# A graph layer on one core: one edge tile in 20 fetched row by row in place of one in 28, and another lead for GpSimd's gathers

## The chip, the core and the metric

The kernel runs on one core of one Trainium2 chip. The metric is the device time of one execution in microseconds; the number of a kernel is the median of its runs. Five engines work side by side, each with its own queue of instructions taken strictly in order: TensorE (PE in the profile; its weight loads have a row of their own, PEld), VectorE (DVE), ScalarE (ACT), GpSimd (POOL) and SyncE (SP). SP, ACT and POOL also issue DMAs; in this kernel ACT does almost nothing else after the first stage.

## What is computed

One layer of a graph network with relations, over 12,500 nodes of 256 features and 212,500 edges that are sorted by their target:

```python
h = jnp.maximum(_layernorm(x, axis=-1), 0.0)
hx = jnp.einsum('ni,rio->rno', h, weight)        # 8 relations
agg = jax.ops.segment_sum(hx[edge_type, src], dst, num_segments=N)
out = x + agg * 0.5**0.5 + h_bias + (h @ loop_weight) * 0.5**0.5
```

## The kernel before

The kernel sums the normalized rows `h[src]` of a target's edges first, for each relation apart, and multiplies by the weights afterwards. The edges are cut into 1583 tiles of at most 128; two tiles make a unit, 128 units make a block of 256 tiles.

**Edge tiles.** For each tile, the 128 rows `h[src]` of 1 KB must be brought from HBM into `msg`, one row to a partition. `edge_sums` (L953) then multiplies them by a one-hot matrix `oh`, which VectorE makes (L935), in four matmuls (L972; 32-bit data), and `add_sums` (L988) lets VectorE add the result of a unit to the ring `acc` of sums (L998). The buffers of `msg` hold 66 tiles.

**Two ways to bring the rows.** Most tiles are *gathered*: `gather` (L871) issues one indirect DMA on GpSimd (L885), which takes the 128 indices of the tile from a column of `gidx`. The others are *fetched*: `single_rows` (L855) picks tile t if `t % SINGLE == SINGLE - 1`, if it lies in block 1 or later, and if `t + AHEAD < NT` (64 and 1583). `begin_fetch` (L860) cuts such a tile into four parts of 32 rows, two for SP's queue and two for ACT's. `load_sources` (L897) loads the 32 row offsets of a part into registers of that engine (L900, a TENSOR_LOAD in the profile), and `fetch_row` (L907) issues a DMA of 1 KB for each row (L908). TensorE waits for a fetched tile's 128 rows on one of four counters ahead of the tile's first matmul (L969).

**Group products.** The nodes stand in 98 groups of 128. When a group's sums are complete, `product` (L1145) multiplies them by the weights (L1154, 36 matmuls a group), and `finish` (L1164) adds them to the rows of `x`, stores four groups at a time on SP (L1173) and begins a group further on. The rows `hr` and `xr` of later groups are loaded on SP (L1104), four groups at a time. The edge indices of the next block are loaded on SP too (L380), and small rows of each block, `spans`, on ACT from block 2 on (L392).

**What sets the order.** The program is written out in one loop over the tiles t (L1316), and each engine takes its own instructions in that order.

- The gathers run ahead of the sums: at step t, tiles up to `goal(t)` (L892) are gathered. The lead is `max(NEXT, AHEAD - max(0, t - NARROW) // SLOPE)`: 64 tiles up to t = 170, then one tile less every 5 tiles, down to `NEXT` = 8 at t = 450, and 8 from there on. A second bound (`STARTED`, `STEEP`) holds it down in the first tiles. Each gather waits for the sums of the last unit ahead of it in the program (L889, "no faster than the sums").
- A fetch begins at step t for tile t + `FAR` = t + 36, or when the gathers reach the tile, where their lead is longer than that. Its parts are put in two lists, to be taken from 8 steps later (`HOLD`), and each step takes up to `FETCH` = 4 entries (a load or a row) from each list (L920). A tile is 66 entries a list, about 17 steps. A buffer of `msg` is given out in the order of these calls, and a row waits until the tile that had the buffer before is summed.
- The stores and loads of the groups, of the indices and of the spans stand between the rows on SP's and ACT's queues where the loop puts them.

Before the loop and in its first part, the rows of x are normalized and written to `h32` in HBM; the first 100 gathers take x itself and normalize in place.

Of the kernel before, what the change touches and what calls it, by code (L numbers as in the profile page):

```python
# [55 lines left out]
STEEP = 2  # L56
NARROW = 170
SLOPE = 5
NEXT = 8

SINGLE = 28
FETCH = 4
SOURCES = 32
BY_SP = (0, 2)
# [175 lines left out]
def kernel(  # L240
# [20 lines left out]
    NT = plan.NT  # L261
# [36 lines left out]
    def place_of(t):  # L298
        u, i = divmod(t, PAIR)
        half = 0 if PAIR * u + 1 == NT else PAIR - 1 - i  # L300
        return u // P, half, u % P


    with ExitStack() as main:
# [550 lines left out]
        def single_rows(t):  # L855

            return (t % SINGLE == SINGLE - 1 and place_of(t)[0] and t + AHEAD < NT
                    and state["h32"] is not None and t // QUAD * QUAD >= state["h32"] + LATE)
# [33 lines left out]
        def goal(t):  # L892

            lead = max(NEXT, AHEAD - max(0, t - NARROW) // SLOPE)
            return min(t + lead + 1, STARTED + STEEP * (t // PAIR * PAIR))

        def load_sources(t, r0, engine):  # L897
# [302 lines left out]
        with tc.manual_schedule():  # L1200
# [115 lines left out]
            for t in range(NT):  # L1316
# [3 lines left out]
                while gathered < min(NT, goal(t)):  # L1320
                    gather(gathered)
                    gathered += 1
# [122 lines left out]
```

## Time and profile before

| what | value |
| --- | --- |
| median of 3 runs | 1996.98 us (1995.14 to 1998.15) |
| the profiled execution | 1995.13 us |
| its span, first to last instruction | 1993.4 us |
| PE busy | 1779.7 us (89%) |
| PEld busy | 1557.2 us (78%) |
| DVE busy | 1378.2 us (69%) |
| POOL busy | 1461.3 us (73%) |
| ACT busy | 136.1 us (7%) |
| mean granted TensorE clock | 0.959 |

How to read it. Times are microseconds from the start of the span; durations of single instructions are often given in nanoseconds. A group's row reads: line, engine, operation, output<-input by the program's names, xcount | busy time, mean ns of one | idle time of the engine ahead of them, and what ended most of that idle time. "issue" there is time in which the engine waited for nothing that the profile shows. A timeline row reads: start, duration, engine, line, operation, names, xcount [idle time before <- what ended it]; neighbouring instructions of one line are merged, and SPq or ACTq stands for an issue queue. A waits row reads: who <- whom: us in total, times, longest. A windows row reads: from:to, length, then busy us (xcount) of each engine that takes part, the granted clock, the share of the DMA engines and GB/s. Issuing a DMA or loading registers is not counted as busy, so ACT and SP can be full while these rows show nothing; their timelines show it.

### The profile page before, as it was taken

How to read it: one execution, taken by the hardware profiler on the slowest of the kernel's cores; microseconds unless marked ns; L12 is line 12 of the kernel's file. 1: busy time of each engine (PE TensorE's matmuls, PEld its weight loads, DVE VectorE, ACT ScalarE, POOL GpSimd, SP SyncE). 2: the span in 40 equal slices, each digit the busy share in tenths (PEclk: the TensorE clock that was granted, in tenths of full speed). 3: DMA queues.
4: the chain of work that ended last, by engine and by line, in shares of the span. 5: the costliest groups of instructions: out<-in, count | busy, mean ns of one | idle time of the engine just before them, and what ended most of it. 6: DMA issues, size and time to landing. Idle time of an engine off the chain costs nothing. (4 is left out here: it accounts for less than half of the span.)

```text
span 1993.4 us, 39889 instructions
## 1 busy us (share of the span) xinstructions
PE 1779.7 (89%) x10171; PEld 1557.2 (78%) x10171; DVE 1378.2 (69%) x3288; ACT 136.1 (7%) x243; POOL 1461.3 (73%) x1563
## 2 busy tenths in 40 slices
PE   2458999999999988999999999999999999899998
PEld 2347899899978876888878887878877887787986
DVE  6779767779856777656569666668766667765752
ACT  6764200000000000000000000000000000000000
POOL 7677777777767777777777777777777777777774
PEclk9559999999999999999999999999999999999999
DMA  8993434444444544444444444444444344444432
GB/s 269 354 289 98 143 106 138 141 136 120 139 119 118 150 130 114 136 130 123 140 119 142 131 119 139 131 129 139 132 121 142 109 141 131 117 142 118 130 106 77
DMA packets 157314, 279.57 MB, mean 140 GB/s; under 512 B 34799, under 2 KB 107864, under 8 KB 157080
## 3 DMA queue, kind: packets, MB, share of 16 engines
q0 software_dynamic: 73824, 201.69, 34.7%
q1 hardware_dynamic: 75896, 72.34, 11.7%
q10 hardware_dynamic: 7360, 2.97, 0.8%
q8 instruction: 80, 1.31, 0.3%
q14 instruction: 154, 1.26, 0.2%
HBM read 251.26 MB, written 25.60 MB: 139 GB/s over the span
## 5 line engine op out<-in xcount | busy, mean ns | idle before, releaser
L885 POOL DMA_INDIRECT msg<-h,gidx x1438 | 1364.7, 949 | 470.0 <-issue 353.8
L972 PEld LDWEIGHTS ps<-oh,msg 128*128 128x128 f32 x6332 | 995.2, 197 | 344.8 <-DMA msg<-h,gidx 206.5
L972 PE MATMUL ps<-oh,msg 128*128 128x176 f32 (+1 forms) x6332 | 1107.2, 305 | 176.2 <-DMA msg<-h,gidx 99.4
L1154 PE MATMUL po<-w,acc 128*128 128x256 f32 x3136 | 883.1, 386 | 9.4 <-DVE acc L998 9.4
L998 DVE TENSOR_TENSOR acc<-acc,ps 128x352 f32 x792 | 409.9, 518 | 369.9 <-PE ps L972 357.8
L1154 PEld LDWEIGHTS po<-w,acc 128*128 128x128 f32 x3136 | 532.1, 192 | 42.8 <-DVE acc L998 11.4
L935 DVE TENSOR_TENSOR oh<-fixed,cols 128x704 f32<-128x704 f32 x397 | 349.2, 880 | 0.0
L1036 DVE SCALAR_TENSOR_TENSOR acc<-types,pt 128x256 f32<-128x256 bf16 (+1 forms) x688 | 247.5, 413 | 85.0 <-PE pt L1018 79.8
L885 POOL DMA_INDIRECT msg<-in_x_dram,gidx x100 | 94.8, 948 | 38.8 <-issue 30.3
L1154 PE MATMUL po<-wl,self_t 128*128 128x256 f32 x392 | 111.7, 409 | 3.4 <-DVE acc L998 1.7
L1154 PEld LDWEIGHTS po<-wl,self_t 128*128 128x128 f32 x392 | 72.0, 205 | 12.9 <-DVE acc L998 2.5
L823 ACT ACTIVATE msg<-msg,shift,rstd 128x256 f32<-128x256 f32 x100 | 50.7, 586 | 4.2 <-DVE shift L820 3.4
L823 ACT ACTIVATE xt<-xt,shift,rstd 128x256 f32<-128x256 f32 x98 | 50.0, 587 | 7.0 <-DVE shift L820 5.6
L1167 DVE TENSOR_TENSOR xr<-xr,po 128x256 f32<-128x256 f32 x98 | 40.5, 414 | 13.3 <-PE po L1154 12.5
L793 DVE BATCH_NORM_STATS2 stats<-xt 128x6 f32<-128x256 f32 x98 | 34.3, 412 | 19.1 <-DMA xt<-in_x_dram 18.3
L1090 DVE CAST types<-pt 128x512 bf16<-128x512 f32 x22 | 15.2, 692 | 44.8 <-PE pt L1086 44.8
L1023 DVE COPY self_t<-pt 128x256 f32<-128x256 f32 x98 | 40.8, 416 | 6.8 <-PE pt L1018 5.5
L1018 PE MATMUL pt<-ident,hr 128*128 128x128 f32 x196 | 38.1, 277 | 7.5 <-DMA hr<-h 6.4
L1168 DVE TENSOR_TENSOR xr<-xr,po 128x256 f32<-128x256 f32 x98 | 41.2, 421 | 3.4
L429 DVE TENSOR_SCALAR moves<-fixed 128x271 int32<-128x271 int32 (+1 forms) x90 | 40.5, 451 | 3.1 <-DVE acc L998 2.1
L431 DVE COPY_PREDICATED fixed<-moves,fixed 128x311 int32<-128x311 int32 (+14 forms) x90 | 38.0, 422 | 3.1
L793 DVE BATCH_NORM_STATS2 stats<-msg 128x6 f32<-128x256 f32 x100 | 34.2, 410 | 0.0
(154 smaller groups left out, 321.1 us busy)
## 6 DMA issues: line engine op xcount, KB each, us to landing
msg<-h SPq DMA_DIRECT2D x2880, 1.0 KB
msg<-h ACTq DMA_DIRECT2D x2880, 1.0 KB
msg<-h,gidx POOLq DMA_INDIRECT x1438
xt<-in_x_dram SPq DMA_DIRECT2D x24, 512.0 KB
h<-xt SPq DMA_DIRECT2D x24, 512.0 KB
xr<-in_x_dram SPq DMA_DIRECT2D x24, 512.0 KB
hr<-h SPq DMA_DIRECT2D x24, 512.0 KB
out_dram<-xr SPq DMA_DIRECT2D x24, 512.0 KB
```

The lines of the kernel that those rows point to most:

```text
L429: nc.vector.tensor_single_scalar(m, packed[:, :n], 1 << (bit + k), op=ALU.bitwise_and)
L793: in_run("stats", nc.vector.bn_stats(stats[:n, k, :], row), row is rows_[-1])
L823: nc.scalar.activation(row, row, AF.Relu, bias=shift[:n, j : j + 1], scale=rstd[:n, j : j + 1])
L885: i = nc.gpsimd.indirect_dma_start(out=msg[t], out_offset=None, in_=table[:, :], in_offset=bass.IndirectOffsetOnAxis(ap=gidx[b][:, at : at ...
L935: j = nc.vector.tensor_tensor(o[:, k : k + v, :i, :], iota_f.unsqueeze(1).unsqueeze(1).to_broadcast([P, v, i, C]), of.unsqueeze(3).to_broa ...
L972: j = nc.tensor.matmul(ps[:, c, :width], m[:, c * P : (c + 1) * P], o[:, :width], start=(i == 0 and c == 0), stop=(end and c == KC - 1))
L998: i = nc.vector.tensor_tensor(a, a, ps, op=ALU.add)
L1023: nc.vector.tensor_copy(got["self", g][:, :, :n], pst[:, :, :n])
L1036: i = nc.vector.scalar_tensor_tensor(acc[:, :, r, s0 : s0 + n], of, float(r + 1), pst[:, :, :n], op0=ALU.is_equal, op1=ALU.mult)
L1154: i = nc.tensor.matmul(got["out", g][:n], lhs, rhs, start=(r == R and c == 0), stop=(r == R - 1 and c == KC - 1))
L1167: nc.vector.tensor_add(rows_[:n, k, :], rows_[:n, k, :], outs[g % 2][:n, 1, :])
L1168: nc.vector.tensor_add(rows_[:n, k, :], rows_[:n, k, :], got["out", g][:n])
```

## The change

Three constants and one line in `goal`:

```diff
-NEXT = 8
-
-SINGLE = 28
+NEXT = 24
+CLOSE = 8
+
+SINGLE = 20
@@ def goal(t):
             lead = max(NEXT, AHEAD - max(0, t - NARROW) // SLOPE)
+            lead = min(lead, max(CLOSE, (NT - t) // SLOPE))
             return min(t + lead + 1, STARTED + STEEP * (t // PAIR * PAIR))
```

The fetched tiles are those with t % 20 == 19, where they were those with t % 28 == 27. The gathers' lead falls from 64 as before, but to 24 tiles, which it has from t = 370 on. Near the end it is (1583 - t) // 5, below 24 from t = 1464 on and 8 from t = 1539 on. Everything else stays, the entries a step, the distance of 36 tiles and the four counters too.

## The prediction, made before the result was known

> **What bounds the kernel now.** I read the page first (its costliest groups and its DMA issues), then a stretch of the timeline, then the waits of all engines, then busy time by window, and last the timelines of the two issue queues, SP's and ACT's.
>
> ```profile
> L885 POOL DMA_INDIRECT msg<-h,gidx x1438 | 1364.7, 949 | 470.0 <-issue 353.8
> msg<-h SPq DMA_DIRECT2D x2880, 1.0 KB
> msg<-h ACTq DMA_DIRECT2D x2880, 1.0 KB
> ```
> ```profile
> 1303.54 0.95 POOL L885 DMA_INDIRECT msg<-h,gidx  x1 [0.30 <-issue]
> 1304.79 0.95 POOL L885 DMA_INDIRECT msg<-h,gidx  x1 [0.31 <-issue]
> ```
> ```profile
> PEld ps L972 <- DMA msg<-h,gidx: 206.5, 315, 3.3
> ```
>
> A gather takes GpSimd 0.95 us, and the next starts 1.25 us after it (1304.79 - 1303.54). TensorE's weight loads wait 206.5 us in all for what GpSimd gathers; of its own waits this is by far the largest. The windows below count L972's matmuls (four to an edge tile) and, in the last row, L885's gathers.
>
> ```profile
> 300.00:420.00 120.00, 74.63 (x456) 71.22 (x456) 1.00 0.48 139
> 600.00:1900.00 1300.00, 738.98 (x4252) 652.04 (x4252) 0.98 0.45 130
> 600.00:1900.00 1300.00, 971.54 (x1026) 0.98 0.45 130
> ```
>
> Early, while GpSimd still has a long lead, 114 tiles pass in 120 us: 1.053 us a tile is TensorE's own pace. From 600 to 1900 us it is 1063 tiles in 1300 us, 1.223 us each, and GpSimd issues 1026 gathers, one in 1.267 us, nearly its 1.25 us. So **GpSimd's issue rate is the bound** of that stage. The 45 fetched tiles (2880 rows of 1 KB on each of SP and ACT, 64 a tile and queue) are what takes load off it. The question is then what a fetched tile costs the two queues.
>
> ```profile
> L900 SPq TENSOR_LOAD <-single x90: 2114/2184/3745, 301.8 to 1858.9; - x90
> L900 ACTq TENSOR_LOAD <-single x90: 2147/2298/3144, 262.7 to 1800.7; - x90
> ```
> ```profile
> 1439.86 23.31 SPq L908 DMA_DIRECT2D msg<-h  x64
> ```
> ```profile
> 701.31 155.65 ACTq L908 DMA_DIRECT2D msg<-h  x384
> ```
>
> On SP one fetched tile is 64 rows with the second value load among them, 23.31 us, and the first load ahead of them, 2.18 us; with some 0.2 us of gaps that is **25.7 us**. On ACT six tiles in a row (384 rows, eleven of their twelve loads inside) took 155.65 us; with the load ahead of them, 2.30 us, and its gap of 0.2 us that is 158.2 / 6 = **26.37 us**. This row has no room for long waits: it has 0.41 us a row, loads included.
>
> Of before, one tile in 28 is fetched: 28 x 1.223 = 34 us between two of them. Both queues fit in it. They are the next resource: 77% full.
>
> **The change, part by part.**
>
> *One in 20.* The fetched tiles are 259, 279, ..., 1499: 63 in place of 45 (the rule needs block 1 or later, so tile 256 at least, and t + 64 < 1583). It takes 18 gathers from GpSimd, 18 x 1.25 = 22.5 us, and adds 18 x 64 = 1152 rows and 36 loads to each queue. If GpSimd stayed the bound, 20 tiles would take 19 x 1.25 = 23.75 us. But each queue needs 25.7 to 26.4 us of pure issue in these 20 tiles. **The queues become the bound**, and TensorE, which takes each tile in order, waits at every fetched tile for its rows.
>
> What else stands on the two queues counts as well:
>
> ```profile
> 1435.28 0.41 SPq L1173 DMA_DIRECT2D out_dram<-xr  x1
> 1435.75 0.51 SPq L1104 DMA_DIRECT2D hr<-h  x1
> 1463.27 0.40 SPq L1104 DMA_DIRECT2D xr<-in_x_dram  x1
> 399.01 0.38 SPq L380 DMA_DIRECT2D nat_s<-in_src_dram  x1
> 387.33 3.81 ACTq L392 DMA_DIRECT2D spans<-in_dst_dram  x8
> ```
>
> SP stores and loads for four groups every 64 tiles: 0.41 + 0.51 + 0.40 us and some 0.25 us of gaps, 1.57 us in 3.2 fetched tiles, 0.49 us each; a block of 256 tiles adds three index loads of about 0.5 us with the gap, 0.12 us a fetched tile. SP's period is 25.7 + 0.6 = 26.3 us. ACT issues 34 span rows (8 in 3.81 us), some 16 us in the whole run, 0.3 us a fetched tile: 26.65 us. Against 23.75 us, that is 1.11 to 1.12 of what GpSimd would need.
>
> *When the queues begin.* A fetched tile's first row waits for its buffer, which the tile 66 places earlier frees.
>
> ```profile
> 337.27 17.55 SPq L908 DMA_DIRECT2D msg<-h  x46
> 370.92 0.42 SPq L1173 DMA_DIRECT2D out_dram<-xr  x1
> 372.07 12.29 SPq L908 DMA_DIRECT2D msg<-h  x29
> ```
> ```profile
> 0.00:315.50 315.50, 151.08 (x772) 141.06 (x772) 0.82 0.66 209
> 0.00:337.30 337.30, 164.86 (x856) 153.90 (x856) 0.83 0.64 203
> 0.00:405.00 405.00, 207.02 (x1116) 194.41 (x1117) 0.86 0.61 192
> ```
>
> Before, tile 279's rows begin at 337.27 us, just when 856 matmuls, tiles 0 to 213, are done. Now the first is tile 259, freed by tile 193: 776 matmuls, at about 316 us. ACT: 64 rows with one load end 24 us later, at 340 us. SP: tile 259 ends at 340, and tile 279's first 46 rows are out by 361; then the store at L1173 waits, as before, for its sums until 371 us, and the last 18 rows (of 29 in 12.29 us, loads included) end at about 378 us. From there SP has no reason to wait: five tiles and 3.6 us of other issues later, 378 + 5 x 25.7 + 3.6, it ends tile 379 at 510 us. TensorE is at tile 279 at 405 us (1116 matmuls) and, at 1.053 us a tile, at tile 379 at 510 us. There it first waits.
>
> *From there to tile 1499* lie 56 periods. SP: 510 + 56 x 26.3 = 1983 us. ACT, with no store in its way: 340 + 62 x 26.37 + 16 = 1991 us. ACT's span rows also wait for DMAs of SP:
>
> ```profile
> 1260.97 27.82 ACTq L392 DMA_DIRECT2D spans<-in_dst_dram  x8
> ```
>
> Eight that took 3.81 us earlier took 27.82 us here. SP was then idle in front of a store and ACT far ahead of it. With both late and abreast, the wait is at most ACT's few us of lead and a landing: none to 24 us a block, four blocks, so 0 to 96 us. I take 6 us in all, near the row of 3.81 us, because SP's store waits for nothing when SP runs behind TensorE. A landing adds 2 us. Tile 1499 is then taken at 1991 + 6 + 2 = **1999 us**.
>
> *The lead.* A lead of 24 in the middle lets GpSimd gather on while TensorE stands at a fetched tile. Its 19 gathers take 23.75 of 26.65 us, so the stalls of TensorE hide them. With a lead of 8, twelve of the next 20 tiles would be gathered after the stall, in 15 us, while TensorE needs 21 us to reach the last of them, so they would be hidden too. I cost the lead at nothing. It gains what GpSimd's waits for the sums were worth only if GpSimd is the bound.
>
> *The end.* At tile 1499 the lead is (1583 - 1499) // 5 = 16, so gathers to tile 1515 are out, and 67 are left.
>
> ```profile
> L885 POOL DMA_INDIRECT msg<-h,gidx x1438: 940/946/1253, 136.4 to 1969.8; - x180
> span 1993.4 us, 39889 instructions
> ```
>
> The last starts 66 x 1.25 = 82.5 us later, and from its start to the span's end it was 1993.4 - 1969.8 = 23.6 us. (TensorE would need 83 x 1.053 = 87 us and its last products; that ends alike.) Span: 1999 + 82.5 + 23.6 + 1 = 2106 us. The profiled execution took 1995.13 us with a span of 1993.4, and the median is 1996.98: 1.7 and 1.9 us more. **Predicted: 2110 us**, 5.7% slower.
>
> For the price of a row when neither queue ever rests, no stretch of before is a pure case. The quickest SP tile bounds it below:
>
> ```profile
> 1635.73 22.99 SPq L908 DMA_DIRECT2D msg<-h  x64
> ```
>
> With its first load, the gaps and the other issues that is 22.99 + 2.18 + 0.2 + 0.6 = 26.0 us. Had ACT no more than that, tile 1499 would come at 512 + 56 x 26.0 = 1968 us and the end near 2079; I take 2075. Above, 0.4 us more in each of 62 tiles and 20 us of span waits give 2155.
>
> **The rivals.**
>
> *GpSimd stays the bound (not slower).* If issuing rows cost the queues under 23.75 us a tile, the 18 gathers go and the longer lead removes some of GpSimd's waits:
>
> ```profile
> POOL msg L885 <- PE ps L972: 46.1, 123, 1.5
> ```
>
> The usual gap of 0.30 us, 123 times, is 37 us of these 46.1, so 9 us can go. 1997 - 22.5 - 9 = **1965 us**. It decides at 23.75 us a fetched tile; every row above is over 25. The Trainium skill, "DMA: Bandwidth & Descriptors", section "Issuing engines are not separate DMA queues", speaks for it: it says that the time to initiate a DMA "is usually small relative to the DMA itself", by which more fetched tiles would be free and the time about 1965 us. The trace disagrees for these transfers: 0.36 us a row of 1 KB on SP, 23.31 us a tile. Chance 5%; that gain and loss cancel within 0.2% needs a period near 24 us: 2%.
>
> *The two queues hold each other up.* If both share something that a row holds for its whole 0.228 us,
>
> ```profile
> L908 ACTq DMA_DIRECT2D msg<-h x2880: 217/228/867, 337.3 to 1813.7; - x192
> ```
>
> then 128 rows need 29.2 us and with part of the loads some 31 us: 512 + 56 x 31 = 2248, and 2360 us at the end. The Trainium skill, "Perfetto Trace Analysis", section "DMA Instruction — HWDGE (DVE, Sync)", says that a sequencer locks a shared descriptor generator for exclusive use, which is such a case. Against it: SP issued through most of ACT's 155.65 us, and the median row stayed at 228 ns. Part of this, or span waits near their upper end, is what lies over 2155: 7%.
>
> *The queues cost less than any row shows* (a period of 24.3 to 25.7 us): 2000 to 2075 us, 4%.
>
> **How the numbers follow.** The forecast, the queues as the bound at about 26.5 us, has 82%, and its own range 2075 to 2155 is the range. Slower: 82 + 7 + 4 = 93%; within 0.2%, about what a measurement of this kernel tells from no change, 2%; faster 5%.
>
> **What would show it.** Right: the L908 rows on both queues run without idle time from about 380 to 1990 us, 64 in some 26.5 us; TensorE's largest wait stands at L972 on fetched tiles, about 56 times, some 5 us each, and ends with a row of SP or ACT, not with a gather; GpSimd's waits on the sums grow, since it now stands at its lead; 20 tiles take some 26.5 us between 600 and 1900, so 981 tiles there in place of 1063. Wrong: 20 tiles in under 24.5 us; queues with gaps; or TensorE still waiting on single gathers. An ACT queue stretched at L392 would show the span waits as dearer than I took them.

## The result, and the profile after

| | before | after |
| --- | --- | --- |
| median of 5 runs | 1996.83 us (1990.56 to 1998.15) | 2217.64 us (2216.19 to 2220.78) |
| the profiled execution, its span | 1995.13, 1993.4 us | 2217.64, 2215.9 us |
| mean granted TensorE clock | 0.959 | 0.896 |

The changed kernel takes 1.1106 times as long [1.1085, 1.1127]. The sign and the bound are those of the prediction, but the loss is twice the forecast one: 221 us where 113 were expected, and 2217.64 lies outside the range of 2075 to 2155.

The page of the changed kernel, its span, two of its costliest groups and the DMA queue that carries ACT's rows. A queue's line gives packets, MB, and share of 16 engines. Lines of code stand one or two further down than before: the gathers are L886, the sums' matmuls L974, the wait on the counters L971, the rows L910.

```profile
span 2215.9 us, 44710 instructions
q10 hardware_dynamic: 9664, 4.15, 1.2%
L886 POOL DMA_INDIRECT msg<-h,gidx x1420 | 1347.8, 949 | 708.5 <-issue 309.4
L974 PEld LDWEIGHTS ps<-oh,msg 128*128 128x128 f32 x6332 | 1056.3, 205 | 479.3 <-PEq L971 321.1
```

GpSimd issues 18 gathers fewer (1420 for 1438) and yet stands idle 708.5 us ahead of them, where it was 470.0. Ahead of TensorE's weight loads the largest idle time no longer ends with a gather but at L971, the wait for a fetched tile's rows ("PEq" is TensorE's own sequencer, which waits there for a counter). Four rows of the waits view of the same kernel (who <- whom: us, times, longest) show where TensorE's weight loads and GpSimd now stand longest:

```profile
PEld ps L974 <- PEq L971: 321.1, 56, 12.2
POOL msg L886 <- issue: 340.7, 1034, 3.8
POOL msg L886 <- DMA msg<-h,gidx: 184.1, 247, 3.1
POOL msg L886 <- PE ps L974: 180.4, 171, 6.4
```

TensorE's waits on single gathers, 206.5 us before, are down to 3.5 us; 56 waits of 5.7 us each on fetched tiles have come. GpSimd waits more for the sums (180.4 us for 46.1), since it stands at its lead while TensorE stands. The third row was not in the prediction at all: GpSimd waits for the landing of gathers that it issued earlier, 184.1 us in all. Its row of before, which the prediction didn't use:

```profile
POOL msg L885 <- DMA msg<-h,gidx: 49.3, 127, 2.0
```

Busy time by window, first L974's matmuls in three stretches, then L886's gathers in the last of them:

```profile
0.00:526.20 526.20, 273.65 (x1517) 257.64 (x1517) 0.88 0.57 174
0.00:2102.70 2102.70, 1064.61 (x5997) 1005.86 (x5998) 0.89 0.45 128
600.00:1900.00 1300.00, 654.94 (x3704) 619.88 (x3704) 0.89 0.42 114
```
```profile
600.00:1900.00 1300.00, 835.16 (x881) 0.89 0.42 114
```

Tile 379 is taken at 526.2 us (1516 matmuls are done before it) and tile 1499 at 2102.7, so the 56 periods between them last 1576.5 us: **28.15 us each**. From 600 to 1900 us 3704 / 4 = 926 tiles pass, where the prediction had 981.

That the queues set this pace is seen on their timelines, first SP's, then ACT's (start, duration, engine, line; the register loads lie inside the rows' durations):

```profile
1339.83 0.41 SPq L1175 DMA_DIRECT2D out_dram<-xr  x1
1340.30 0.69 SPq L1106 DMA_DIRECT2D hr<-h  x1
1341.08 34.49 SPq L910 DMA_DIRECT2D msg<-h  x80
1375.63 0.40 SPq L1106 DMA_DIRECT2D xr<-in_x_dram  x1
```
```profile
742.48 12.49 ACTq L393 DMA_DIRECT2D spans<-in_dst_dram  x8
1104.88 3.85 ACTq L393 DMA_DIRECT2D spans<-in_dst_dram  x8
1108.82 347.19 ACTq L910 DMA_DIRECT2D msg<-h  x825
```

There is no gap here between the rows and the stores and loads beside them: SP goes from one to the next within 0.1 us. ACT issues 825 rows, 12.9 tiles, in one piece of 347.19 us, 0.421 us a row with its loads. The piece of before that the prediction used, 384 rows in 155.65 us, had 0.405. Whole runs of both queues (first and last start):

```profile
L910 ACTq DMA_DIRECT2D msg<-h x4032: 217/228/746, 316.9 to 2079.4; - x192
L910 SPq DMA_DIRECT2D msg<-h x4032: 227/228/1958, 317.0 to 2089.4; - x192
```

SP ends 10 us behind ACT, and for 49 of the 57 tiles from 379 on the last row issued is SP's, so it is mostly SP's rows that TensorE waits for. One stall, at tile 979, in TensorE's timeline and in SP's up to the last row of that tile:

```profile
1374.00 0.93 PEld L974 LDWEIGHTS ps<-oh,msg 128*128 128x128 f32 x4 [9.43 <-PEq L971]
```
```profile
1357.99 5.86 SPq L910 DMA_DIRECT2D msg<-h  x18
```

The last row has been issued at 1357.99 + 5.86 = 1363.85 us and the tile is taken at 1374.00. **This row needed some 10 us to land**, not the 2 us of the prediction. Over the 57 tiles the median from the end of SP's last row to the tile's first weight load is 11.0 us.

### The profile page after: what moved, and what is told of

It reads as the page before. It is cut to its first block, busy times and chain, and to the rows that moved or that the text cites. A ratio compares the mean times of both kernels' runs of the same rounds, so it can differ in the third digit from the quotient of the medians.

```text
span 2215.9 us, 44710 instructions
## 1 busy us (share of the span) xinstructions
PE 1800.9 (81%) x10171; PEld 1640.4 (74%) x10171; DVE 1378.6 (62%) x3288; ACT 136.0 (6%) x243; POOL 1444.4 (65%) x1545
## 3 DMA queue, kind: packets, MB, share of 16 engines
q10 hardware_dynamic: 9664, 4.15, 1.2%
## 5 line engine op out<-in xcount | busy, mean ns | idle before, releaser
L886 POOL DMA_INDIRECT msg<-h,gidx x1420 | 1347.8, 949 | 708.5 <-issue 309.4
L974 PE MATMUL ps<-oh,msg 128*128 128x176 f32 (+1 forms) x6332 | 1119.3, 310 | 376.4 <-PEq L971 300.5
L974 PEld LDWEIGHTS ps<-oh,msg 128*128 128x128 f32 x6332 | 1056.3, 205 | 479.3 <-PEq L971 321.1
L1156 PE MATMUL po<-w,acc 128*128 128x256 f32 x3136 | 916.0, 398 | 10.6 <-DVE acc L1000 10.6
L1156 PEld LDWEIGHTS po<-w,acc 128*128 128x128 f32 x3136 | 554.0, 200 | 46.8 <-DVE acc L1000 12.6
L886 POOL DMA_INDIRECT msg<-in_x_dram,gidx x100 | 94.8, 948 | 40.1 <-issue 31.3
L1020 PEld LDWEIGHTS pt<-ident,hr 128*128 128x128 f32 x196 | 26.6, 153 | 10.5 <-DMA hr<-h 7.0
```

Of the source, the lines that this page charges most:

```text
L886: i = nc.gpsimd.indirect_dma_start(out=msg[t], out_offset=None, in_=table[:, :], in_offset=bass.IndirectOffsetOnAxis(ap=gidx[b][:, at : at ...
L974: j = nc.tensor.matmul(ps[:, c, :width], m[:, c * P : (c + 1) * P], o[:, :width], start=(i == 0 and c == 0), stop=(end and c == KC - 1))
L1020: in_run("turns", nc.tensor.transpose(pst[:, c, :n], rows_[:n, c * P : (c + 1) * P], ident[:n, :n]), c == KC - 1)
L1156: i = nc.tensor.matmul(got["out", g][:n], lhs, rhs, start=(r == R and c == 0), stop=(r == R - 1 and c == KC - 1))
```

## The experiments

What stood to be settled is where the second hundred microseconds come from. That the issue of the queues is the bound was common to all theories. They differ in why a fetched tile costs 28.1 us and not 26.6. **Theory A**, in some expectations, is that a row costs its issuer what it costs, whatever else runs. **Theory B:** rows and gathers get into each other's way behind the queues, in the DMA engines; with one of the two gone, the rows cost what they cost before. **Theory C:** SP and ACT hold up each other at the issue, whether GpSimd gathers or not (the prediction's second rival, in a mild form). A further rival is that the new lead, not the fetching, costs the time. Of each edit only the main lines are shown.

Kernels that ran together share their runs of before, and each ratio is against those. The sets ran on different chips, and on three of them before itself takes 2397 to 2424 us: instructions reach all queues late there (last section). Times are therefore compared within a set; periods of a tile, which come from the traces, are compared only where that lateness doesn't show.

**The two parts of the change, and the size and shape of a row** (before: 2423.73 us).

Only one tile in 20, the lead as before (against the kernel before):

```diff
-SINGLE = 28
+SINGLE = 20
```

> One tile in 20 fetched, the lead as before (8 tiles). If the two issue queues are the bound, as predicted, the lead does not matter: 2205 to 2230 us, the same 28.1 us from fetched tile to fetched tile. If the longer lead is what makes rows dearer (more gathers in flight beside them), a large part of the 107 us beyond the prediction goes: 2110 to 2160 us.

Measured: 2787.95 us, 1.150 [1.1456, 1.1545].

Only the lead (against the changed kernel, as all edits below but that of e9):

```diff
-SINGLE = 20
+SINGLE = 28
```

> One tile in 28 fetched, the lead 24 tiles and 8 at the end. GpSimd's issue rate stays the bound: 1980 to 1997 us (its waits for the sums, some 9 us beyond the usual gap, can go). If gathers far ahead slow the rows or the sums, it is slower than 2000 us.

Measured: 2432.98 us, 1.0041 [1.0023, 1.006]. The fetching has nearly all of the loss. On this chip every row was late; SP's timeline in this kernel:

```profile
1041.45 50.96 SPq L910 DMA_DIRECT2D msg<-h  x78
```

That is 0.65 us a row with its loads, where 0.36 was usual. So the sizes of this set say little about the other chip.

Rows of 512 bytes. The second half of each fetched row is left out, and the matmuls use the first in its place:

```diff
-msg[t][r0 + i : r0 + i + 1, :].bitcast(U8), h32_bytes[:, bass.ds(v, D * 4)])
+msg[t][r0 + i : r0 + i + 1, :P].bitcast(U8), h32_bytes[:, bass.ds(v, P * 4)])
```

> The changed kernel with rows of 512 bytes: a fetched tile brings only the first half of each row, and its matmuls use that half twice, so instructions are as many. Theory A (a row costs its issuer what it costs, or the two issuers hold a shared generator): nothing changes, 2205 to 2230 us, a row pair still about 0.35 us on each queue. Theory B (all rows of both queues run on one DMA engine, which backs up into the queues): that engine has less to move, and the time falls to 2100 to 2170 us, with rows near 0.33 us.

Measured: 2770.15 us, 1.1427 [1.1383, 1.1471].

The row written as four pieces of 256 bytes, so that several DMA engines might share it:

```diff
+    msg[t][r0 + i : r0 + i + 1, :].bitcast(U8).rearrange("p (a b) -> p a b", a=4),
+    h32_bytes[:, bass.ds(v, D * 4)].rearrange("p (a b) -> p a b", a=4))
```

> The changed kernel with each row of 1 KB described as four pieces of 256 bytes, which should run on four DMA engines. Theory B: the backlog behind one engine goes, rows come back to 0.32 us, the period to 26 to 26.7 us, the time to 2090 to 2130 us, and the wait from the last row to the tile's first matmul falls from 10 us to 3 us. Theory A: four pieces cost the issuer as much as one or more: 2210 us or over.

Measured: 2770.28 us, 1.1427 [1.1384, 1.1471]. Neither tells anything here, for the late instructions hide what the rows themselves cost. Both were run again in the next set. Beside e1, though, they bear on the lead: e5 is the changed kernel in all but the form of a row, and beside it the old lead costs 17.7 us more (2787.95 - 2770.28; 2785.57 to 2790.32 against 2768.67 to 2771.9).

**The changed kernel again, both row forms, and one tile in 24** (before: 1995.33 us).

> The changed kernel itself, as the control of this set. On a chip on which the kernel before takes about 1997 us: 2217 us, ratio 1.11. On one like that of the first set, where it took 2424 us and every queue's instructions came late: a ratio of 1.14 to 1.15.

Measured: 2215.19 us, 1.1103 [1.1071, 1.1135]: the result repeats.

> As in the first set (rows of 512 bytes; the second half of each fetched row is left out and the first used twice). Theory A, a row costs its issuer what it costs: within 0.5% of the control. Theory B, one DMA engine serves all rows and backs up: 2 to 5% below the control where the kernel before takes about 1997 us; nothing where the issuers are late anyway, since no backlog forms there.

Measured: 2211.36 us, 1.1084 [1.105, 1.1118]. The page's queue line and two rows of the waits from 1500 to 1700 us:

```profile
q10 hardware_dynamic: 9664, 2.09, 1.0%
```
```profile
PEld ps L974 <- DMA msg<-h,gidx: 53.2, 60, 2.5
POOL msg L886 <- DMA msg<-h,gidx: 38.4, 39, 2.0
```

Half the bytes (2.09 MB for 4.15 on ACT's queue) bring 0.2%, within what the runs scatter. **The loss doesn't go with the bytes.** Theory B as it stood there, an engine with less to move, had 2 to 5% and missed. In that stretch TensorE again waits on single gathers and GpSimd for their landing; over the whole run TensorE stands 184.2 us at 36 fetched tiles and 151.2 us on gathers, and GpSimd 266.8 us for landings (184.1 in the changed kernel). So fetching and gathering are slowed together.

> As in the first set (each row in four pieces of 256 bytes, meant for four DMA engines). Theory B: 4 to 6% below the control on a chip like the prediction's, with rows back at 0.32 us and the tile's first matmul 3 us after its last row. Theory A: at the control or slower.

Measured: 2217.09 us, 1.1112 [1.108, 1.1145]. The queue has the same 9664 packets and 4.15 MB as in the changed kernel: the four pieces went out as one again. The run shows nothing but the changed kernel once more, and whether spreading a row over engines helps stays untried.

One tile in 24 with the new lead:

```diff
-SINGLE = 20
+SINGLE = 24
```

> One tile in 24 fetched, with the changed kernel's lead. A fetched tile then has 23 x 1.25 = 28.75 us of gathers beside it, a little over the 28.1 us that the queues need in the changed kernel, so both bounds nearly meet: 1985 to 2010 us, ratio 0.994 to 1.007. If the queues' need grows with the load on them or what stands on them bunches, up to 2040 us.

Measured: 2040.72 us, 1.023 [1.0201, 1.0259]: slower, and above the range expected; it meets the 2040 us named for a need that grows with the load. The matmuls from 600 to 1900 us, and two waits of the whole run:

```profile
600.00:1900.00 1300.00, 726.99 (x4113) 639.32 (x4112) 0.97 0.45 125
```
```profile
PEld ps L974 <- DMA msg<-h,gidx: 219.2, 309, 4.4
POOL msg L886 <- DMA msg<-h,gidx: 112.6, 203, 3.4
```

Now the queues are not the bound: 4113 / 4 = 1028 tiles make 30.3 us for 24 tiles, above the 28.1 us that a fetched tile costs, and TensorE's waits end with gathers. But 23 gathers in 30.3 us are 1.32 us each in place of 1.25. **More rows make the gathers dearer too**, before they fill the queues. It shows as GpSimd's waits for the landing of gathers, 112.6 us for 49.3.

**Rows alone, gathers alone, one queue** (before: 2423.7 us, a chip with late instructions).

No gathers from tile 460 on; the sums take a fixed tile in place of the gathered rows, so that part of the input is left out:

```diff
+            if t >= 460 and not single_rows(t):
+                kind[t] = "h"
+                msg[t] = still
+                return
```

> The changed kernel without any gather from tile 460 on: those tiles are multiplied from one fixed tile instead, and only the fetched tiles still bring rows. Theory B, now: rows and gathers meet in one DMA engine, rows stand 7 us in its queue, and that backs up into SP and ACT and makes every gather land late. Without gathers rows cost 0.32 us again and SP needs some 26 us a fetched tile: 2080 to 2115 us. Theory C: SP and ACT slow each other's issue (something shared that a row holds), gathers or not: 2200 to 2220 us. (Where the kernel before takes 2424 us, instructions are late on all queues and neither is told apart.)

Measured: 2270.54 us, 0.9359 [0.931, 0.9408]. The first 460 tiles ran at this chip's late pace, and the total misses the expectation by that; what counts is the stretch without gathers. L979's matmuls and waits from 800 to 2000 us, SP's timeline and ACT's:

```profile
800.00:2000.00 1200.00, 627.51 (x3604) 593.79 (x3603) 0.92 0.09 26
```
```profile
PEld ps L979 <- PEq L976: 202.2, 44, 9.3
```
```profile
1302.49 49.04 SPq L915 DMA_DIRECT2D msg<-h  x128
```
```profile
1218.03 337.68 ACTq L915 DMA_DIRECT2D msg<-h  x825
```

Both queues are full and still the bound (44 stalls), and 20 tiles take 1200 / (3604 / 4) x 20 = **26.64 us**. The prediction's price was 26.65. ACT issues its 825 rows in 337.68 us, 9.5 us less than in the changed kernel. From SP's last row to the tile's first weight load the median is 2.0 us. Theory C falls in its plain form: SP and ACT don't hold each other up without gathers. Also the lateness of this chip's instructions is gone in this stretch: rows come at 0.38 us each on SP, where e2 had 0.65.

ACT's half of each fetched tile left out (the sums take 64 rows of it, and SP loads its half alone):

```diff
-BY_SP = (0, 2)
+BY_SP = (0, 1)
-            for k, r in enumerate(range(0, P, SOURCES)):
+            for k, r in enumerate(range(0, P // 2, SOURCES)):
```

> The changed kernel with ACT's half of each fetched tile left out: SP brings 64 rows and the tile's matmuls use these 64 partitions. Theories B and C both: SP's rows go back to about 0.32 us and its period to some 26.1 us: 2080 to 2115 us; under B gathers also land in 3 to 5 us again. If SP's price comes from SP alone, it stays at 28 us and 2200 to 2220 us.

Measured: 2631.29 us, 1.0846 [1.0773, 1.092], with this chip's lateness in it. No rows at all (a fixed tile in place of each fetched one):

> The changed kernel with its 63 fetched tiles not fetched at all: they are multiplied from one fixed tile, and no row is issued. Both theories: GpSimd is the bound with a gather in 1.25 us, since nothing delays their landing: 1940 to 1975 us, which is what the change would give if fetching were free. If it stays above 1990 us, gathers are slowed by something other than the rows.

Measured: 2294.08 us, 0.9456 [0.9409, 0.9504]; with the lateness too. Both were run again.

One tile in 32 with the lead of before:

> The kernel before with one tile in 32 fetched, its lead kept. If rows delay gathers already at one in 28 (median wait in before small, the tail long), the six extra gathers (7 us) are paid back in part: 1990 to 2003 us, ratio 0.998 to 1.004. If not: 2003 to 2006 us.

Measured: 2404.58 us, 0.9909 [0.9878, 0.9941], below the ratio expected.

**The same on a chip without lateness** (before: 1990.71 us).

> As before (ACT's half of each fetched tile left out). Where the kernel before takes about 1997 us: theory B (rows and gathers share one DMA engine) has 64 rows a tile there in place of 128: SP's rows at 0.32 to 0.33 us, a period of 26 to 26.6 us, gathers landing in 3 to 6 us, 2085 to 2125 us. If SP's 28.1 us come from its own row DMAs beside the gathers, whoever else issues: 2190 to 2220 us.

Measured: 2125.06 us, 1.0667 [1.0638, 1.0696], the upper end of theory B's range. L975's matmuls by window, SP's timeline at the place shown of the changed kernel, and two waits:

```profile
600.00:1900.00 1300.00, 684.47 (x3912) 646.42 (x3912) 0.92 0.40 117
```
```profile
1294.52 31.27 SPq L910 DMA_DIRECT2D msg<-h  x80
```
```profile
PEld ps L975 <- PEq L971: 231.3, 58, 8.8
POOL msg L886 <- DMA msg<-h,gidx: 4.9, 16, 0.3
```

With gathers but one queue the period is 1300 / (3912 / 4) x 20 = **26.58 us**, and 80 rows take 31.27 us where they took 34.49. GpSimd's waits for the landing of gathers fall from 184.1 to 4.9 us, and from SP's last row to the tile's first weight load it is 1.6 us in the median, where it was 11.0. The run takes away one queue and half of the rows at once; which of the two it is, no run here separates.

> As before (the 63 tiles not fetched, multiplied from one fixed tile, no row issued). Where the kernel before takes about 1997 us: with no rows, every gather lands on all sixteen DMA engines in about 3 us, GpSimd issues one in 1.25 us: 1940 to 1975 us. If gathers are slow for another reason than the rows (1.4 us each or more): over 2100 us.

Measured: 1945.77 us, 0.9767 [0.9741, 0.9793]. The gathers (L890) by window:

```profile
600.00:1900.00 1300.00, 983.96 (x1038) 0.98 0.43 126
```

That is one gather in 1.252 us, the 1.25 us of the prediction, with nothing to disturb it. Fetching for nothing would give 1946 us; the prediction's first rival had 1965.

> As before (one tile in 28, the changed lead). Where the kernel before takes about 1997 us: 1985 to 2000 us, ratio 0.994 to 1.002, so that the lead has no part in the slowdown. Over 2005 us would mean that gathers further ahead slow the rows.

Measured: 1982.91 us, 0.9956 [0.9937, 0.9975]: the lead alone gains a little and has no part in the loss.

> As before (one tile in 32, the lead of before). Where the kernel before takes about 1997 us: 1990 to 2006 us. Where it takes 2424 us: 2400 to 2410 us again, since the queues are the bound there at one in 28 already.

Measured: 1980.4 us, 0.9944 [0.9922, 0.9965], below what was expected. The rows' cost to the gathers shows in one wait of this kernel:

```profile
POOL msg L885 <- DMA msg<-h,gidx: 31.4, 103, 0.3
```

Fewer fetched tiles (39 for 45) mean six gathers more, 7.5 us, and still a kernel that is 10 us faster. No wait for a landing is longer than 0.3 us now, which is GpSimd's usual gap; before, the 127 waits held some 11 us beyond that gap (49.3 - 127 x 0.30). That pays for the six gathers; the rest of the gain is not accounted for.

**Both together** (before: 2397.48 us, late instructions). One tile in 32, and one in 30, each with the new lead:

> The changed kernel's lead with one tile in 32 fetched (39 tiles). With rows that cost nothing to others it would be the kernel without rows plus 24 gathers: 1946 + 24 x 1.25 = 1976 us. The little that rows at one in 32 still delay adds 0 to 6 us: 1974 to 1982 us, ratio 0.991 to 0.996, faster than both kernels. If the gains of the lead and of one in 32 are the same gain, it stays at 1980 us; if they add, 1972 us.

Measured: 2378.07 us, 0.9929 [0.9913, 0.9946].

> The same with one tile in 30 (42 tiles): 1946 + 21 x 1.25 = 1972 us without any delay by rows, and more delay than at one in 32: 1974 to 1982 us. If the delay by rows falls off slowly with their number, 1978 us or more; if it is gone by one in 30, 1973 us.

Measured: 2381.29 us, 0.9936 [0.992, 0.9952]. Both beat before, neither the other, and neither shows more than e9 did on a chip of this kind. They were not run on a chip without lateness; there the fastest that stands is e9b, though its runs (1978.27 to 1981.82 us) touch those of e2b (1980.68 to 1984.87).

## Why the sign was right and the size was not

The table sets the periods of a fetched tile side by side; the two in the middle are the ones that settle it.

| kernel | rows on | gathers | us per 20 tiles |
| --- | --- | --- | --- |
| changed (600 to 1900 us) | SP and ACT | yes | 28.1 |
| e8b (600 to 1900 us) | SP | yes | 26.6 |
| e6 (800 to 2000 us) | SP and ACT | no | 26.6 |
| prediction | SP and ACT | yes | 26.3 (SP), 26.65 (ACT) |

- **What binds** was right: TensorE stalls at L971 on 56 fetched tiles, the queues have next to no gaps, GpSimd stands at its lead.
- **When it begins** was nearly right: the first fetched row starts at 317.0 us (316 forecast), and tile 379 is taken at 526.2 us, 14 us after the forecast 512. SP issues its last row at 516.4 us, 6 us late; the landing, 9.7 us and not the 2 of "a landing adds 2 us", is the other 8.
- **The step that failed** is the price of a fetched tile, "the queues as the bound at about 26.5 us". It was read from stretches of before in which the queues rested a quarter of the time, and a full queue comes close to it as long as either the other queue or the gathers are gone (26.6 us in e8b and in e6). With two full queues beside the gathers it is 28.15 us. Over 56 periods that is 89.5 of the 110 us by which the span missed (2215.9 for 2106, with 1999 - 512 = 1487 us forecast for these periods, 26.55 each). The term that was mis-sized is SP's: the prediction had 26.3 us for SP and let ACT, at 26.65, set the pace. That e6 agrees with 26.65 is luck in part, for there too SP's rows came last.
- **The end** took 113.2 us from tile 1499 (2215.9 - 2102.7) for 107; e8b has 113.3, so the rows of two queues aren't the reason. GpSimd's last gather starts at 2192.7, 90 us after that tile for 82.5, for it waited some 8 us for sums.
- **The span rows** on ACT, taken at 6 us of waits with up to 96 possible, took 12.49 us for eight once and 3.85 once, and ACT, not the later queue, stood 17 us ahead of the last two (1812.88 to 1829.80 us): without weight there. SP, the later one, stood 14.0 us in two waits that the waits view ends with a DMA of span rows, which the prediction had at nothing.
- **The lead**, costed at nothing, has little weight: 0.9956 and 1.0041 alone on two chips. With one tile in 20 it hides something: e1 lost 17.7 us against e5 on one chip.
- **The bounds of the range** hold a slip: by its own terms the lower one comes to 2077 us at the end, not 2079. It has no weight.
- **The rivals.** That GpSimd stays the bound fell at its own condition, 23.75 us a tile. That "the two queues hold each other up" was a part of the truth: two queues are dearer than one, by 1.5 us a tile and not by 4.5, but only beside gathers. For that rival the prediction had named the Trainium skill, "Perfetto Trace Analysis", section "DMA Instruction — HWDGE (DVE, Sync)", a sequencer that locks a shared descriptor generator; e6, with 26.64 us for two full queues, speaks against it as the cause by itself.

Why the loss nearly doubled from an error of 6% in one price: the loss per period is the difference of two close numbers. Twenty tiles took 20 x 1.223 = 24.46 us before, so it is 2.1 us forecast (26.55 - 24.46) and 3.7 measured (28.15 - 24.46), over 56 periods 117 and 207 us.

**Where rows and gathers meet.** The runs show that the rows are not slowed without gathers (e6), that neither side is with one queue of rows (e8b) or none (e7b), and that both are with two full queues; half the bytes save nothing (e4b). The trace's single packets point further. A row is one packet of 1024 bytes. From the end of its issue on ACT to the start of its packet pass 2.8 us in the mean before (600 to 1900 us), 6.9 us in the changed kernel (the same stretch), and 0.78 us in e6 without gathers (800 to 2000 us). In the changed kernel packets of ACT's rows run during only some 3% of the time of SP's row packets (13 to 20% when one series is shifted against the other by up to 7 us), as if one DMA engine had them all. In turn, the last of the 16 parts of a gather lands some 4.7 us (median, 600 to 1900 us) after the gather begins before, 7.7 us in e3 and 10.4 us in the changed kernel, but 2.8 us in e8b and in e7b; the 15th lands at 2.7 to 2.8 us in all five. One of 16 parts is late, then, and the whole gather waits for it. The gathers use eight completion semaphores in turn, so GpSimd stands once a landing takes over 8 x 1.25 = 10 us: the third row of the waits. The Trainium skill, "DMA: Bandwidth & Descriptors", section "Why a DMA increments its semaphore by 16 and not by 1", says that the number of engines is the largest, up to 16, that divides the slowest dimension of more than one element on both sides, that a scalar gets one, that such DMAs of SP and ACT take the lowest-numbered engines, and that software can split a contiguous row so that it is spread. The trace lists each row's DMA as one element of 1024 bytes, and its single packet agrees with one engine; the trace doesn't number the engines, and e5b did not spread the row. That it is one engine is therefore argued and not shown. On SP most of the 1.5 us a tile stands in the rows' own DMA instructions: they take 0.251 us in the mean in the changed kernel (600 to 1900 us) and 0.234 us before, in e8b and in e6 (800 to 2000 us), which makes 64 x 0.017 = 1.1 us. SP's two waits on span rows, 14.0 us over the 46 fetched tiles of that stretch, are another 0.3. How a late packet would lengthen them is open; no run here shows it.

## What to carry to other kernels

A price read from a resource that rests a quarter of the time need not hold when it is full beside others: here it was too low. Where the loss is a difference of two close rates, that error comes back multiplied. Before giving one queue the work of another, look at what they share behind the issue: here the landing of both kinds of transfer told it (the waits of GpSimd for its own gathers were in the profile before, 49.3 us, and the row was passed over). Move the ratio the other way as well: one tile in 32 was faster than one in 28, by 0.6%.

## What the hardware showed beyond that

- Many single-row DMAs and indirect DMAs beside each other: SP's last row of a tile needs some 11 us to land and the gathers' last part 10.4 us, with the DMA engines busy only 42% of the time (0.42, the windows' number ahead of the GB/s). With rows on one queue alone it is 1.6 and 2.8 us.
- The chips of these runs differ by a fifth for the same kernel: before took 1990.71 and 1995.33 us on two and 2397.48, 2423.7 and 2423.73 on three. On the latter the queues' instructions come late: 0.65 us a row in e2 for 0.36, and TensorE's weight loads of the sums stood 236.2 us with nothing on record that they waited for, where the same kernel on another chip (e2b) had 4.3 us. In e6 the lateness went with the gathers: 128 rows in 49.04 us, 0.38 us each. Why chips differ is open. The Trainium skill, "DMA: Bandwidth & Descriptors", section "Issuing engines are not separate DMA queues", calls the time to initiate a DMA usually small relative to the DMA itself; for rows of 1 KB on two queues the issue was the bound of the changed kernel, at 0.431 us a row with its loads on SP (34.49 us for 80) and 0.421 on ACT.
- TensorE was granted a lower clock in the kernels in which it stalled at regular intervals: 0.89 from 600 to 1900 us in the changed kernel, 0.98 before, 0.92 in e8b. The periods show no cost of it: 20 tiles take 26.6 us in e8b and in e6, as the queues' own issue does.
